# A recurrent stage with one PSUM bank for each gate and a single set of banks, rows set behind their chain's last step, and a first sample in four buffers

## The chip, the cores and the metric

The kernel runs on one core of one Trainium2 chip. The metric is the device time of one execution in microseconds (us), given as the median of several runs. Kernels are compared by the ratio of their fast runs on the same chip in the same rounds. A profile is one execution taken by the hardware profiler. Its times agree with the timed runs, but one profile differs from the next, mostly late in the program where nothing was changed: from the first difference of the adder convolution (explained below) to the end, the 14 profiles of this case take 6934 to 6973 us. So the argument uses marks inside the first 960 us, and the medians for the whole. All runs were in the fast state.

## The reference, cut to what matters

The program is four layers in a chain on an input of 16 x 32 x 128 x 128, each with a group normalisation before it and a residual after it. The change touches layer 0 and the beginning of layer 1.

```python
# layer 0: a recurrence over the 128 columns of the skewed image
xs = skewed input, moved so that one step is one column            # (128, 16, 128, 128)
def step(carry, xt):
    pc, ph = carry
    ph_shift = pad(ph, one row down)
    g = xt + einsum(W1_prev, ph_shift) + einsum(W1_cur, ph) + b1
    o, f, i, gg = sigmoid, sigmoid, sigmoid, tanh of the four quarters of g
    nc = f * pc + i * gg
    nh = o * tanh(nc)
    return (nc, nh), nh
x = x + scan(step)(_gn(x))
# layer 1: input quantised to 8 bits, then an "adder" convolution
qx = round(clip(_gn(x) / scale, -127, 127))
y  = -sum over the 3 x 3 x 32 patch of |patch - weight|
x = x + y * scale
# layers 2 and 3 (a Hartley convolution and a small U-net) are not touched
```

In step t only the first t + 1 rows have their own input; the rows below are all alike. So the kernel computes only `rows` rows, more with every eight steps.

## The kernel before

The batch of 16 samples is worked on as four groups of 128 partitions (4 samples x 32 channels). Two groups make one **chain**, so there are two independent chains, and the kernel takes a step of one, then of the other. Eight steps are a **chunk**; within a chunk the number of rows is fixed: 10 in the first chunk, 18 in the second, 128 in the last. A tile of one chain step is two groups wide, so at 98 rows the profile shows 196 columns. A **bank** is a piece of PSUM, the memory that TensorE's products go to; here each bank holds two gates of a chain.

One chain step is: TensorE makes 8 products of the input (`xn`) and 16 of the last state (8 of `h`, 8 of `e`, a copy of `h` with its two halves of partitions exchanged), all on 64 x 64 tiles of the array. (The trace has two matmul records for each of these products: 4096 of `xn` for 256 chain steps of 8.) ScalarE takes four gates. VectorE makes the cell and, after ScalarE's tanh of the cell, `h` and `e`.

```python
    T = 8
    F, I, G, O = range(4)
    BANK = ((I, F), (O, G))
    ...
        def add(ch, res, g, half):                 # residual and its statistics, once for each step
            ...
            nc.vector.tensor_add(r, r, h[:, :, 1 : n + 1])
            if n < H:
                r = res[:, g, steps, n:]
                nc.vector.tensor_add(r, r, bcast(h[:, :, n], 2, H - n))
            nc.vector.bn_stats(stat1[:, g, 2 * ch + half, :], ...)
            ...
        with tc.tile_pool(name="s0_gps", bufs=2, space=PSUM) as gps:
            for ch in range(NT):
                n = rows(ch)
                following = load(ch + 1) if ch + 1 < NT else None
                if ch:                             # rows that come in with this chunk
                    m = rows(ch - 1)
                    for c in range(2):
                        for v in (hs[c][(ch - 1) % 2][:, T - 1, :, 1:], ex[c][0][:, :, 1:], cs[c]):
                            if n > m:
                                nc.vector.tensor_copy(v[:, :, m:n], bcast(v[:, :, m - 1], 2, n - m))
                for j in range(T):
                    t = T * ch + j
                    for c in range(2):
                        ...
                        pg = gps.tile([128, 2, 2, 2, H], F32, name=f"pg{c}")   # two banks, two gates in each
                        place = {q: pg[:, i, k] for i, b in enumerate(BANK) for k, q in enumerate(b)}
                        ...                        # 8 products of xn, then 16 of h and e
                        for q in (F, I, G, O):
                            nc.scalar.activation(gt[:, q, :, :n], place[q][:, :, :n], ...)
                        nc.vector.tensor_mul(cell, cell, gt[:, F, :, :n])
                        nc.vector.tensor_mul(ig[:, :, :n], gt[:, I, :, :n], gt[:, G, :, :n])
                        nc.vector.tensor_add(cell, cell, ig[:, :, :n])
                        nc.scalar.activation(th[:, :, :n], cell, AF.Tanh)
                        nc.vector.tensor_mul(h_out[:, :, 1 : n + 1], gt[:, O, :, :n], th[:, :, :n])
                        for half in range(2):      # e: the halves of h exchanged
                            nc.vector.tensor_copy(ex[c][(t + 1) % 2][own, ...], h_out[other, ...])
                    if j >= T // 2:
                        add(ch, res, j - T // 2, 0)
                        if following:
                            normalise(ch + 1, following[0], j - T // 2)
                    elif ch:
                        add(ch - 1, previous, j, 1)
```

This is the source order. Unless it is told otherwise, the compiler chooses the order in which each engine's queue holds the instructions. The kernel has a helper, `keep_order`, which ties each instruction to the one before it on its engine. Before and after, it is not used in this stage.

The next stage quantises sample 0 in four pieces, with two buffers for the pieces and two for the quantised results, writes them to memory and reads the whole map back from there:

```python
        for i in range(4):
            t = self.unquantised(0, i)     # load a 512 KB piece
            self.scaled(0, t)              # ScalarE
            self.quantise(0, i, t)         # VectorE, then a store to memory
            weave.due(float("inf"))
        before, following = None, self.loaded(0, 0)    # the map
```

## Time and profile before

| mark of the profile before | us |
|---|---|
| median of the timed runs given with it (3 runs, 7895.84 to 7903.62) | 7900.34 |
| span of the profile | 7884.7 |
| recurrent stage: first tanh begins | 104.5 |
| first four chunks (10 to 34 rows) | 155.3 |
| chunk at 98 rows | 51.51 |
| last `h` begins | 837.15 |
| first load of sample 0 issued | 839.98 |
| map of sample 0 issued | 900.78 |
| first difference of the adder convolution begins | 934.73 |

The length of a chunk is counted from the first tanh of the cell in it to the first in the next; tiles of each chunk have their own width, so the trace tells them apart.

The page gives the busy share of each engine in 40 equal slices, in tenths. In the views PE is TensorE, PEld its weight loads, DVE VectorE, ACT ScalarE, and SPq the queue that issues transfers. A slice is 7884.7 / 40 = 197 us, so the recurrent stage and the first sample lie in the first five digits.
```profile
PE   3788366566677668886676666897667765997797
DVE  7787599989969797887877978888787877134213
```
The reader is to see that no engine of this stretch stands at 9, and that the fifth digit dips: 3 for TensorE and 5 for VectorE. That dip, at 788 to 985 us, holds the wait for the first sample.

### The profile page before, as it was taken

The numbers are of one execution on the slowest core, as the hardware profiler recorded it, in microseconds if no ns is written. First come the engines' busy times: TensorE is split into PE (matmuls) and PEld (weight loads), VectorE is DVE, ScalarE is ACT, GpSimd is POOL, SyncE is SP. The second block draws the span as 40 slices with busy tenths as digits, with TensorE's granted clock in tenths as the row PEclk, the third lists the DMA queues.
The fourth block names the chain that finished last, engine by engine and source line by source line (L and its number), as shares of the span: only waits on it lengthen the run. The fifth ranks groups of instructions, "written<-read, shape, count | busy, mean of one in ns | idle before, by whom it ended". The sixth has DMA issues, their size and how long they took to land. (4 is left out here: it accounts for less than half of the span.)

```text
span 7884.7 us, 258419 instructions
## 1 busy us (share of the span) xinstructions
PE 5635.8 (71%) x121132; PEld 3165.4 (40%) x121132; DVE 5847.9 (74%) x7177; ACT 5406.7 (69%) x3129; POOL 21.6 (0%) x15
## 2 busy tenths in 40 slices
PE   3788366566677668886676666897667765997797
PEld 3665222222253334442343343343335333555564
DVE  7787599989969797887877978888787877134213
ACT  2565488799869879887778877887887885123122
POOL 0000000000000000000000000000000000000000
PEclk9899788888878779998868788998787887897896
DMA  8653111111132431112332432120333233434314
GB/s 319 223 181 130 59 50 60 48 52 39 50 116 80 123 102 51 58 33 67 79 98 90 129 89 73 40 70 34 88 86 101 87 102 94 116 107 122 91 33 90
DMA packets 374269, 721.68 MB, mean 92 GB/s; under 512 B 50896, under 2 KB 219856, under 8 KB 362320
## 3 DMA queue, kind: packets, MB, share of 16 engines
q1 hardware_dynamic: 372768, 704.58, 29.4%
q8 instruction: 949, 15.55, 0.8%
q14 instruction: 120, 0.98, 0.0%
q10 hardware_dynamic: 432, 0.57, 0.0%
HBM read 507.21 MB, written 164.32 MB: 85 GB/s over the span
## 5 line engine op out<-in xcount | busy, mean ns | idle before, releaser
L610 ACT ACTIVATE d_act<-q,neg 128x8192 f16<-128x8192 f16 (+1 forms) x612 | 4332.5, 7137 | 930.9 <-PE acc L536 877.6
L614 DVE TENSOR_SCALAR d_dve<-q,qw 128x8192 f16<-128x8192 f16 (+1 forms) x1692 | 3906.2, 2361 | 512.0 <-PE acc L536 476.3
L536 PE MATMUL acc<-d_dve,sel 128*32 128x512 f16 x27072 | 2007.5, 432 | 861.6 <-DVE d_dve L614 838.8
L536 PEld LDWEIGHTS <-sel 128*32 128x32 f16 x36864 | 1121.1, 106 | 2800.6 <-issue 2196.8
L536 PE MATMUL acc<-d_act,sel 128*32 128x512 f16 x9792 | 784.5, 446 | 499.1 <-ACT d_act L610 494.7
L1519 PE MATMUL acc<-xp,wf 32*32 32x512 f32 x25600 | 986.0, 625 | 29.0 <-issue 16.1
L1519 PEld LDWEIGHTS acc<-xp,wf 32*32 32x32 f32 x25600 | 478.8, 105 | 378.1 <-issue 244.6
L1458 ACT ACTIVATE y<-pooled,b 32x128 f32<-32x128 f32 x512 | 204.6, 400 | 532.2 <-DVE pooled L1444 525.1
L223 PE MATMUL pg<-h,wb 64*64 64x20 f32 (+15 forms) x4096 | 401.2, 323 | 102.4 <-DVE h L255 67.0
L753 PE MATMUL acc<-y,u_conv 32*32 32x256 f32 (+1 forms) x9728 | 402.2, 511 | 79.3 <-issue 35.8
L223 PE MATMUL pg<-e,wb 64*64 64x20 f32 (+15 forms) x4096 | 353.2, 318 | 24.7 <-DVE e L258 10.0
L243 ACT ACTIVATE gt<-pg,bias 128x20 f32<-128x20 f32 (+15 forms) x1024 | 302.7, 377 | 84.2 <-PE pg L223 80.0
L1204 PE MATMUL acc<-xp 32*64 32x204 f32 (+3 forms) x8576 | 247.3, 368 | 130.0 <-ACT xp L1170 107.8
L552 PE MATMUL acc<-q,sel 32*32 32x512 f16 x4608 | 158.6, 556 | 204.9 <-DVE xr L519 115.1
L223 PEld LDWEIGHTS pg<-h,wb 64*64 64x64 f32 x4096 | 243.7, 156 | 140.5 <-DVE h L255 97.6
L223 PEld LDWEIGHTS pg<-e,wb 64*64 64x64 f32 x4096 | 250.6, 158 | 108.3 <-DVE e L258 77.9
L223 PE MATMUL pg<-xn,wb 64*64 64x8 f32 (+60 forms) x4096 | 267.9, 304 | 25.3 <-ACT gt L243 17.4
L1616 ACT ACTIVATE xr<-xr,l_ms 128x1024 f32<-128x1024 f32 x64 | 70.4, 1141 | 305.6 <-DVE xr L1611 254.3
L753 PEld LDWEIGHTS acc<-y,u_conv 32*32 32x32 f32 x9728 | 189.7, 119 | 220.0 <-issue 126.5
L1164 ACT ACTIVATE xp<-xp,fr_shift,stats 128x1280 f32<-128x1280 f32 (+1 forms) x128 | 181.7, 1431 | 136.1 <-DMA xp<-x_d 73.9
L1204 PEld LDWEIGHTS acc<-xp 32*64 32x64 f32 (+1 forms) x8576 | 199.3, 147 | 187.8 <-ACT xp L1170 118.0
L254 ACT ACTIVATE th<-c 128x20 f32<-128x20 f32 (+15 forms) x256 | 81.9, 320 | 222.2 <-DVE c L252 221.2
(203 smaller groups left out, 4247.9 us busy)
## 6 DMA issues: line engine op xcount, KB each, us to landing
xr<-x_d SPq DMA_DIRECT2D x192, 512.0 KB
xp<-x_d SPq DMA_DIRECT2D x112, 640.0 KB
q<-q_d SPq DMA_DIRECT2D x32, 2145.0 KB
x_d<-xr SPq DMA_DIRECT2D x128, 512.0 KB
x_in<-in_x_dram SPq DMA_DIRECT2D x16, 2048.0 KB
res<-in_x_dram SPq DMA_DIRECT2D x64, 512.0 KB
xn<-in_xs_dram SPq DMA_DIRECT2D x64, 512.0 KB
xn<-xn SPq DMA_DIRECT2D x128, 256.0 KB
```

The source lines that it names most:

```text
L223: nc.tensor.matmul(place[q][64 * pair : 64 * pair + 64, :, :width], wb[half, 4 * kind + KIND[q]].rearrange("p b o -> p (b o)"), v[half], s ...
L243: nc.scalar.activation(gt[:, q, :, :n], place[q][:, :, :n], AF.Tanh if q == G else AF.Sigmoid, bias=bias[:, KIND[q] : KIND[q] + 1],)
L254: nc.scalar.activation(th[:, :, :n], cell, AF.Tanh)
L536: self.nc.tensor.matmul(acc[k][32 * j : 32 * j + 32, :], self.sel16[:, i // 9, :], d[:, row : row + 4, c : c + W], start=False, stop=i == 71,)
L552: self.nc.tensor.matmul(acc[k][32 * j : 32 * j + 32, :], self.sel16[rows, 8, :], q[rows, row : row + 4, kw : kw + W], start=tap == 0, stop ...
L610: nc.scalar.activation(dst, src, AF.Relu, bias=self.neg[:, i : i + 1])
L614: nc.vector.tensor_scalar(dst, src, self.qw[:, i : i + 1], 0.0, ALU.subtract, ALU.max)
L753: nc.tensor.matmul(acc[blk][32 * j : 32 * j + 32, o : o + rows * n], t[part, 4 * par + tap, :], src[part, top : top + rows, left : left + ...
L1164: nc.scalar.activation(v, v, AF.Identity, bias=shift[0], scale=self.stats3[:, 1])
L1204: nc.tensor.matmul(gram[blk][j : j + width, at : at + n], xp[part, l, 2 + j : 2 + j + width], xp[part, rows, j : j + width + 4], start=sta ...
L1458: nc.scalar.activation(d, s, AF.Identity, bias=bj)
L1519: nc.tensor.matmul(acc[blk][32 * j : 32 * j + 32, :], tap_of("all", tap)[rows], xp[rows, 4 * j + kh : 4 * j + kh + 4, kw : kw + W], start= ...
```

## The change

It has several parts. Each gate gets a bank of its own, F and I are produced first, and so ScalarE can begin while TensorE still writes G and O. Since one set for both chains now takes eight banks, as many as two sets took before, the input products of a chain's next step are placed behind the other chain's step. The rows that come in with a chunk are set right after their own chain's last step instead of at the seam, and the next chunk is normalised two steps sooner. And the first sample's four loads go out at once into four buffers.

```diff
-    BANK = ((I, F), (O, G))
+    PAIRS = ((F, I), (G, O))
 ...
-        with tc.tile_pool(name="s0_gps", bufs=2, space=PSUM) as gps:
+        with tc.tile_pool(name="s0_gps", bufs=1, space=PSUM) as gps:
+            bank = [[gps.tile([128, 2, 256], F32, name=f"pg{c}_{q}") for q in range(4)] for c in range(2)]
+            def product(c, kind, q, copy, pair, v, width): ...      # into bank[c][q]
+            def inputs(c, t, xn): ...                               # 8 products of xn for chain c, step t
+            inputs(0, 0, xn)
             for ch in range(NT):
 ...
-                if ch:                                              # copies of rows at the seam
-                    ...
+                        for gates in PAIRS:
+                            for kind in range(2):                   # h, then e
+                                for copy, q in enumerate(gates):
+                                    for pair in range(2):
+                                        product(c, kind, q, copy, pair, v, n)
+                        if c == 0:
+                            inputs(1, t, xn)
+                        elif t + 1 < W:
+                            inputs(0, t + 1, xn if j + 1 < T else following[0])
 ...
+                        if j == T - 1 and n < H:
+                            m = rows(ch + 1)
+                            for v in (h_out[:, :, 1:], e_out[:, :, 1:], cs[c]):
+                                nc.vector.tensor_copy(v[:, :, n:m], bcast(v[:, :, n - 1], 2, m - n))
+                    if following and 2 <= j < 6:
+                        normalise(ch + 1, following[0], j - 2)
                     if j >= T // 2:
                         add(ch, res, j - T // 2, 0)
-                        if following:
-                            normalise(ch + 1, following[0], j - T // 2)
 ...
-        for i in range(4):
-            t = self.unquantised(0, i)
-            self.scaled(0, t)
-            self.quantise(0, i, t)
-            weave.due(float("inf"))
+        with tc.tile_pool(name="s1_x0", bufs=4, side="right") as pool:
+            xq = [self.unquantised(0, i, pool) for i in range(4)]
+            for i in range(4):
+                self.scaled(0, xq[i])
+                self.quantise(0, i, xq[i])
+                weave.due(float("inf"))
```

More of the change, by code (lines that the diff above doesn't have):

```diff
@@ L199, in stage0, with product, inputs @@
             normalise(0, xn, g)
-        with tc.tile_pool(name="s0_gps", bufs=2, space=PSUM) as gps:
+        with tc.tile_pool(name="s0_gps", bufs=1, space=PSUM) as gps:
+            bank = [[gps.tile([128, 2, 256], F32, name=f"pg{c}_{q}") for q in range(4)] for c in range(2)]
+            def product(c, kind, q, copy, pair, v, width):
+                half = slice(64 * (pair ^ copy), 64 * (pair ^ copy) + 64)
+                nc.tensor.matmul(
+                    bank[c][q][64 * pair : 64 * pair + 64, :, :width],
+                    wb[half, 4 * kind + KIND[q]].rearrange("p b o -> p (b o)"),
+                    v[half],
+                    start=kind == 2,
+                    stop=kind == 1,
+                    skip_group_check=True,
+                )
+            def inputs(c, t, xn):
+                for gates in PAIRS:
+                    for copy, q in enumerate(gates):
+                        for pair in range(2):
+                            v = xn[copy][:, 2 * c : 2 * c + 2, t % T, : t + 1]
+                            product(c, 2, q, copy, pair, v, t + 1)
+            inputs(0, 0, xn)
             for ch in range(NT):
@@ L203, in stage0 @@
                 following = load(ch + 1) if ch + 1 < NT else None
-                if ch:
-                    m = rows(ch - 1)
-                    for c in range(2):
-                        for v in (hs[c][(ch - 1) % 2][:, T - 1, :, 1:], ex[c][0][:, :, 1:], cs[c]):
-                            if n > m:
-                                nc.vector.tensor_copy(v[:, :, m:n], bcast(v[:, :, m - 1], 2, n - m))
                 for j in range(T):
@@ L215, in stage0 @@
                         h_out, cell = hs[c][ch % 2][:, j], cs[c][:, :, :n]
-                        pg = gps.tile([128, 2, 2, 2, H], F32, name=f"pg{c}")
-                        place = {q: pg[:, i, k] for i, b in enumerate(BANK) for k, q in enumerate(b)}
-                        def product(kind, k, i, pair, v, width):
-                            q = BANK[i][k]
-                            half = slice(64 * (pair ^ i), 64 * (pair ^ i) + 64)
-                            nc.tensor.matmul(
-                                place[q][64 * pair : 64 * pair + 64, :, :width],
-                                wb[half, 4 * kind + KIND[q]].rearrange("p b o -> p (b o)"),
-                                v[half],
-                                start=kind == 2 and k == 0,
-                                stop=kind == 1,
-                                skip_group_check=True,
-                            )
-                        for k in range(2):
-                            for i in range(2):
-                                for pair in range(2):
-                                    product(2, k, i, pair, xn[i][:, 2 * c : 2 * c + 2, j, : t + 1], t + 1)
-                        for k in range(2):
+                        for gates in PAIRS:
                             for kind in range(2):
-                                for i in range(2):
+                                for copy, q in enumerate(gates):
                                     for pair in range(2):
-                                        product(kind, k, i, pair, h_in[i][:, :, 1 - kind : n + 1 - kind], n)
+                                        v = h_in[copy][:, :, 1 - kind : n + 1 - kind]
+                                        product(c, kind, q, copy, pair, v, n)
[3 more added lines that the diff above has]
+                            inputs(0, t + 1, xn if j + 1 < T else following[0])
                         gt = gp.tile([128, 4, 2, H], F32, name=f"gt{c}")
@@ L244, in stage0 @@
                                 gt[:, q, :, :n],
-                                place[q][:, :, :n],
+                                bank[c][q][:, :, :n],
                                 AF.Tanh if q == G else AF.Sigmoid,
@@ L255, in stage0 @@
                         nc.vector.tensor_mul(h_out[:, :, 1 : n + 1], gt[:, O, :, :n], th[:, :, :n])
+                        e_out = ex[c][(t + 1) % 2]
                         for half in range(2):
                             own, other = slice(64 * half, 64 * half + 64), slice(64 - 64 * half, 128 - 64 * half)
-                            nc.vector.tensor_copy(ex[c][(t + 1) % 2][own, :, 1 : n + 1], h_out[other, :, 1 : n + 1])
+                            nc.vector.tensor_copy(e_out[own, :, 1 : n + 1], h_out[other, :, 1 : n + 1])
+                        if j == T - 1 and n < H:
[4 more added lines that the diff above has]
+                        normalise(ch + 1, following[0], j - 2)
                     if j >= T // 2:
                         add(ch, res, j - T // 2, 0)
-                        if following:
-                            normalise(ch + 1, following[0], j - T // 2)
                     elif ch:
@@ L477, in __init__, with unquantised @@
             )
-    def unquantised(self, b, i):
-        t = self.xp.tile([128, 8 * W], F32, name="xq")
+    def unquantised(self, b, i, pool=None):
+        t = (pool or self.xp).tile([128, 8 * W], F32, name="xq")
         self.nc.sync.dma_start(t, jc_rows(self.d["x1"], b, i // 2, 8 * (i % 2), 8))
```

## The prediction

> **What bounds the kernel now.** I began with the page. Its slices show three busy engines and no single bound over the whole span, so the place of the change decides. The line groups put every line of the diff except one into the first 840 us: the recurrent stage (its last h is written at 837.2 us) and, at 840 to 935 us, the loading and quantising of the first sample of the next stage. The other 6950 us run the same instructions before and after; I take them as unchanged.
>
> The second view is the timeline of VectorE in the recurrent stage, here where a step is 2 x 98 rows wide. Columns: start, duration, engine, line, operation, tiles, shape, count, and in brackets the idle time before it and what ended it.
> ```profile
> 601.83 0.53 DVE L258 COPY e<-h 64x196 f32<-64x196 f32 x2
> 602.39 0.36 DVE L250 TENSOR_TENSOR c<-c,gt 128x196 f32<-128x196 f32 x1
> 602.67 0.35 DVE L251 TENSOR_TENSOR ig<-gt 128x196 f32<-128x196 f32 x1
> 603.06 0.36 DVE L252 TENSOR_TENSOR c<-c,ig 128x196 f32<-128x196 f32 x1
> 603.92 0.36 DVE L255 TENSOR_TENSOR h<-gt,th 128x196 f32<-128x196 f32 x1 [0.49 <-ACT th L254]
> 604.38 0.53 DVE L258 COPY e<-h 64x196 f32<-64x196 f32 x2
> 604.94 0.36 DVE L250 TENSOR_TENSOR c<-c,gt 128x196 f32<-128x196 f32 x1
> ```
> From one L250 to the next is 604.94 - 602.39 = 2.55 us, one step of one of the two chains. No bracket stands before L250 or L251: VectorE does not wait for a gate here. It waits once, 0.49 us for the tanh of the cell; all else is its own six instructions, in order, the two chains taking turns. So in the wide steps **VectorE's order is the bound**, not the gates.
>
> The third view, the timeline of PE and ScalarE around it, shows what the change wants to shorten.
> ```profile
> 602.41 0.38 PE L223 MATMUL pg<-e,wb 64*64 64x196 f32 x2
> ...
> 603.62 0.33 PE L223 MATMUL pg<-e,wb 64*64 64x196 f32 x2
> ...
> 604.06 1.37 ACT L243 ACTIVATE gt<-pg,bias 128x196 f32<-128x196 f32 x4 [0.18 <-PE pg L223]
> ```
> The four gates start at 604.06, only when the last product has ended (603.62 + 0.33 = 603.95). They are done with F by 604.06 + 1.37/4 = 604.40, and VectorE takes F at 604.94: 0.5 us of slack already.
>
> The fourth view is the table of waits of VectorE from 95 to 841 us: total us, times, longest.
> ```profile
> DVE h L255 <- ACT th L254: 85.9, 196, 1.4
> DVE c L250 <- ACT gt L243: 36.3, 39, 9.3
> DVE ig L251 <- ACT gt L243: 4.7, 26, 0.3
> ```
> Waits for gates are 41.0 us in all, of which 9.3 is the one at the very start. The same table by stretches puts 19.4 + 2.9 + 5.1 + 6.6 = 34.0 us of the 36.3 before 320 us, in steps at most about 50 rows wide. That caps what faster gates can give: 41.0 - 9.3 = about **32 us**.
>
> The fifth view is the timeline after the stage: one 512 KB piece of the first sample after another.
> ```profile
> 855.30 0.56 SPq L482 DMA_DIRECT2D xq<-x_d  x1
> 867.35 1.24 ACT L486 ACTIVATE xq<-xq,shift,r 128x1024 f32<-128x1024 f32 x1 [13.95 <-DMA xq<-x_d]
> 868.62 0.69 DVE L493 TENSOR_SCALAR qt<-xq 128x1024 f16<-128x1024 f32 x1 [11.98 <-ACT xq L486]
> ...
> 870.47 0.53 SPq L482 DMA_DIRECT2D xq<-x_d  x1
> ...
> 900.78 0.53 SPq L505 DMA_DIRECT2D q<-q_d  x1
> ```
> Each load is issued only after the store of an earlier piece on the same issuing queue, and that store waits for its quantised piece. A round is 870.47 - 855.30 = 15.2 us, of which 12.05 us (855.30 to 867.35) is the load. All compute engines stand idle meanwhile; this time is on the path.
>
> **What the Trainium skill says.** (1) "PSUM — Partial Sum Buffer", section "Summary: rules for kernel authors": read PSUM during matmuls from a different bank, and guard by bank. One bank per gate allows F to be read while G is written. The trace before shows the opposite arrangement: ScalarE starts after the last product. (2) Same page, section "Engine vs sequencer instructions": the queues of ScalarE and VectorE are strict FIFO. The trace agrees: F is done at 604.40, but its multiply starts at 604.94, after the two copies ahead of it; so an earlier F does not move it. (3) "TensorEngine Tiling (Array Packing)", section "Key Properties": tiles work in parallel. The trace agrees: h and e products run in each other's time. (4) "DMA: Bandwidth & Descriptors", section "Why a DMA increments its semaphore by 16 and not by 1": a transfer runs on the largest number of engines, up to 16, that divides its slowest dimension on both sides, the lowest-numbered ones on this issuing path. These loads have a slowest dimension of 4 in memory, so 4 engines, always the same. The windows table agrees: a DMA share of 0.25 whether one or two transfers are in flight.
> ```profile
> 860.00:862.00 2.00, 0.00 (x0) 0.00 (x0) 0.00 (x0) 0.00 (x0) 0.00 (x0) 0.50 0.25 92
> 862.00:864.00 2.00, 0.00 (x0) 0.00 (x0) 0.00 (x0) 0.00 (x0) 0.00 (x0) 0.50 0.26 104
> ```
> The last two columns are DMA share and GB/s.
>
> **The change part by part.**
>
> *One bank per gate, F and I first.* The 16 recurrent products of a chain step stay 16, the 8 input products 8, the activations 4. F's and I's products end half-way: at 98 rows the products after e take 603.95 - 602.41 = 1.54 us, so F can start about 0.7 us sooner, and since F and I no longer stand in front of G, G ends near one activation (0.34 us) after its products instead of three (1.03 us). The loop of a single chain shrinks by 0.7 us or a little more. But the compiled order of VectorE is nearly the same: h follows directly on the cell's add 172 times before and 177 times after, and F's multiply directly on a copy of e 163 and 159 times. From 58 rows on PE's order is regular in both programs as well. In the wide steps the 0.7 us go into slack: **0 us**. In the narrow steps, up to about 50 rows, some of the 32 us of gate waits go. There the compiled order is rougher than before: runs of four h products on the same two tiles, then four e products (50 runs of four at 10 rows, 8 at 50, none from 58), where the kernel before always alternates in twos. That loses tile parallelism. I choose a bit under half: **14 us** of 32.
>
> *Inputs behind the other chain's step, a single set of banks.* They now wait for that gate's activation of the same chain's last step. In the wide steps PE has about 0.4 us idle per 2.55 us, and the activations end well before the next h of that chain. **0 us**, with risk in the narrow steps (counted in the choice above).
>
> *Rows set behind their chain's last step.* 90 copies before (30 for each of c, h and e, 165 to 178 ns each), 15 seams x 2 chains x 3 = 90 after: nothing is saved, they move. PE's weight loads waited 39.1 us for such copies, but these waits lie at the seams of chunks beside VectorE's adds. **0 to 3 us**; I count 0.
>
> *Normalising two steps earlier.* Moves 64 activations of 0.84 us median on ScalarE, which has room. **0 us**.
>
> *First sample in four buffers.* Removes three waits for a free buffer and queue place. It does not remove bytes: four loads of 524 KB and four stores of 266 KB on the same four engines. In the compiled order loads 2 to 4 stand behind the issue of the weights' load (846.9 us) and the zero rows, so they can be issued from about 847 to 850. Until the quantised map can be loaded, loads 2, 3, 4 and stores 1, 2, 3 must pass: 3 x 0.524 + 3 x 0.266 = 2.37 MB. Rate: between 856 and 866 the kernel before moved one load and one store, 0.79 MB, in 9.7 us = 81 GB/s; peaks are 104. So 23 to 29 us, plus 2 us that I allow for the last store to land: the map's load goes out at about 847 + 26 + 2 = 875 instead of 900.78. **26 us**.
>
> Sum: 14 + 26 = 40 us, 7900.34 - 40 = 7860.
>
> **The rivals.** (a) *The stage is latency-bound throughout, and each step gains 0.7 us per chain loop*: 128 steps x 0.7 = 90 us, with the first sample 7785. For it: ScalarE waits 221.2 us for the cell. Against it: no gate wait of VectorE beyond 320 us worth more than 1 us, and the unchanged order. (b) *The single set of banks becomes a new wait*: PE, in order, stands before an input product for an activation while the other chain's products queue behind. If 0.3 us were lost in each of some 80 narrow chain steps, 24 us go and the stage loses 10: 7884. For it: the compiled order puts such inputs between the h and e products in narrow steps. Against it: VectorE's own copies of e (0.36 us) hide most of it. (c) *The loads just queue on their four engines and the gain vanishes*: at 81 GB/s or less with the map's first load pushed behind piece 4, gain about 15: 7871. (d) *Loads spread well, and ScalarE and VectorE alone bound the pieces* (1.24 + 1.13 us each): the map goes out near 860, gain 40: 7846.
>
> **Range and chances.** Low: gates 25 and first sample 40 plus a few us from the seams, 7832. High: gates 0, first sample 15, 7886. Runs before differ by 8 us. A gain over 2% would need 158 us, more than VectorE's 126.9 us of waits listed above and the first sample's part together can plausibly give; a loss over 2% has no part to come from. Faster 0.02, same 0.97, slower 0.01.
>
> **What would show it.** After: steps at 98 rows still 2.5 to 2.6 us from F's multiply to the next, with ScalarE's F and I now starting while PE still writes G and O; h still waiting about 0.5 us for the tanh, about 80 to 90 us in all; waits of F's multiply for gates down from 36 to some 22 us; the stage ending near 823 instead of 837 us; the map's load issued 35 to 45 us after the first piece's load instead of 61, DMA share 0.25 throughout. I am wrong if the wide step gets shorter than 2.4 us (VectorE's order was not the bound), if VectorE's gate waits grow (rival b), or if the map goes out less than 15 us sooner relative to the first load.

## The result

The changed kernel took **7879.22 us** in the median (7872.24 to 7884.26, 4 runs) against 7898.16 us for the kernel before (7895.84 to 7903.62, 4 runs). The ratio is 0.9974, with a 95% interval of 0.9957 to 0.9992. Here and below a ratio is the mean time of one kernel's fast runs over that of the other's of the same rounds, so it is not quite the ratio of the medians. The outcome is inside the range of the prediction, but the gain is 19 us where 40 had been predicted.

The views that the prediction used, now of the changed kernel. First VectorE's timeline at 98 rows (start, duration, engine, line, operation, tiles, shape, count, idle time before it and what ended it):
```profile
600.97 0.36 DVE L251 TENSOR_TENSOR c<-c,gt 128x196 f32<-128x196 f32 x1
...
602.50 0.36 DVE L256 TENSOR_TENSOR h<-gt,th 128x196 f32<-128x196 f32 x1 [0.49 <-ACT th L255]
...
603.53 0.36 DVE L251 TENSOR_TENSOR c<-c,gt 128x196 f32<-128x196 f32 x1
```
A step is 603.53 - 600.97 = 2.56 us against 2.55, and the only wait in it is still 0.49 us for the tanh. Then TensorE and ScalarE in the same step:
```profile
602.10 0.37 ACT L255 ACTIVATE th<-c 128x196 f32<-128x196 f32 x1 [0.92 <-DVE c L253]
602.21 0.33 PE L207 MATMUL pg<-e,wb 64*64 64x196 f32 x2
...
602.37 1.35 ACT L244 ACTIVATE gt<-pg,bias 128x196 f32<-128x196 f32 x4
```
The gates begin at 602.37, before the last product of `e` ends (602.21 + 0.33 = 602.54). So the new layout does what it is meant to do, but by only 0.17 us: ahead of the gates stands the other chain's tanh, for which ScalarE waits 0.92 us. VectorE takes F at 603.53, 1.16 us after the gates have begun.

VectorE's waits from 95 to 841 us (total us, times, longest):
```profile
DVE h L256 <- ACT th L255: 83.1, 188, 0.8
DVE c L251 <- ACT gt L244: 23.9, 40, 2.9
DVE ig L252 <- ACT gt L244: 22.0, 46, 3.3
```
The waits of F's multiply fell from 36.3 to 23.9 us, but those of the multiply of I and G rose from 4.7 to 22.0, so the waits for gates went from 41.0 to 45.9 us in all. The wait at the very start has to be taken out of these sums before they are compared. Before, it is one wait of F, 9.3 us; after, it stands in three pieces, at 96.95 and 100.04 us for F (2.43 and 2.91 us) and at 103.56 us for I and G (3.33 us). Without it F's waits fell from 27.0 to 18.6 us, those of I and G rose from 4.7 to 18.7, and the sum from 31.7 to 37.2 us.

The first sample, from the timeline:
```profile
842.11 0.59 SPq L489 DMA_DIRECT2D xq<-x_d  x1
...
861.42 15.84 SPq L505 DMA_DIRECT2D q_d<-qt  x4
...
869.91 1.24 ACT L493 ACTIVATE xq<-xq,shift,r 128x1024 f32<-128x1024 f32 x1 [3.78 <-DMA xq<-x_d]
...
880.12 0.54 SPq L512 DMA_DIRECT2D q<-q_d  x1
...
917.61 9.21 DVE L622 TENSOR_SCALAR d_dve<-q,qw 128x8192 f16<-128x8192 f16 x4 [39.86 <-DMA q<-q_d]
```
The last piece is scaled at 869.91, and the map goes out at 880.12, which is 38.0 us after the first load instead of 60.8. From its issue to its use the map then takes 917.61 - 880.12 = 37.5 us, where it had taken 934.73 - 900.78 = 33.9. DMA share and GB/s stand last in the table of windows:
```profile
862.00:864.00 2.00, 0.00 (x0) 0.00 (x0) 0.96 (x6) 0.00 (x0) 0.00 (x0) 0.50 0.26 106
```
The share is 0.26 although two loads and one or two stores are in flight: still four of the sixteen engines.

| mark, us | before | after | difference |
|---|---|---|---|
| first four chunks (10 to 34 rows) | 155.3 | 162.6 | +7.3 |
| from there to the last `h` | 577.3 | 572.6 | -4.7 |
| chunk at 98 rows | 51.51 | 51.34 | -0.2 |
| last `h` begins | 837.15 | 839.24 | +2.1 |
| from the last `h` to the first difference | 97.6 | 78.4 | -19.2 |
| from there to the end | 6950 | 6953 | +3 |

So the whole gain lies behind the last `h`. The recurrent stage did not get shorter.

### The profile page after: what moved, and what is told of

Read it like the earlier page. It is cut to its first block, busy times and chain, and to the rows that moved or that the text cites. A ratio compares the mean times of both kernels' runs of the same rounds, so it can differ in the third digit from the quotient of the medians.

```text
span 7870.4 us, 258146 instructions
## 1 busy us (share of the span) xinstructions
PE 5674.4 (72%) x121132; PEld 3192.7 (41%) x121132; DVE 5847.9 (74%) x7177; ACT 5407.7 (69%) x3129; POOL 21.9 (0%) x15
## 5 line engine op out<-in xcount | busy, mean ns | idle before, releaser
L207 PE MATMUL pg<-xn,wb 64*64 64x28 f32 (+61 forms) x4096 | 285.0, 302 | 9.8 <-ACT gt L244 3.3
```

Source lines behind the costliest of these rows:

```text
L207: nc.tensor.matmul(bank[c][q][64 * pair : 64 * pair + 64, :, :width], wb[half, 4 * kind + KIND[q]].rearrange("p b o -> p (b o)"), v[half], ...
```

## The experiments

Two theories stood at the beginning. **Theory**: the 14 us that had been expected in the narrow steps are really there, and the compiled order of TensorE's products eats them; the wide steps are bound by VectorE's order. **Rival**: the single set of banks is a wait of its own (rival b of the prediction), or the two chains are bound by their own latency, so that nothing on VectorE helps.

All kernels below gave correct results. Each was timed in rounds with the kernel before, whose medians were 7896.1 us in the first two jobs, 7871.0 in the job of the ninth and tenth and 7877.7 in that of the last two. The columns to the right come from one profile each.

| kernel | median us (runs) | ratio to before, 95% interval | first four chunks | chunk at 98 rows | last `h` begins | last `h` to first difference |
|---|---|---|---|---|---|---|
| before | | 1 | 155.3 | 51.51 | 837.15 | 97.6 |
| after | 7879.22 (4) | 0.9974, 0.9957 to 0.9992 | 162.6 | 51.34 | 839.24 | 78.4 |
| e1_first4 | 7874.24 (9) | 0.9973, 0.9963 to 0.9983 | 155.6 | 52.63 | 844.01 | 77.4 |
| e2_recurrent | 7899.78 (13) | 1.0000, 0.9991 to 1.0009 | 162.0 | 51.36 | 840.21 | 96.9 |
| e3_pe_order | 7854.80 (5) | 0.9947, 0.9935 to 0.9960 | 141.2 | 51.34 | 816.46 | 78.5 |
| e4_spread16 | 7853.14 (5) | 0.9939, 0.9926 to 0.9951 | 162.0 | 51.36 | 840.23 | 43.6 |
| e5_all_order | 7895.96 (13) | 0.9998, 0.9990 to 1.0007 | 151.8 | 52.46 | 859.71 | 77.7 |
| e6_fill | 7783.37 (4) | 0.9856, 0.9841 to 0.9871 | 131.1 | 44.66 | 740.91 | 78.7 |
| e7_fill_spread | 7741.59 (4) | 0.9804, 0.9788 to 0.9820 | 129.2 | 44.66 | 739.52 | 43.4 |
| e8_step_order | 7875.83 (7) | 0.9975, 0.9964 to 0.9985 | 153.5 | 51.33 | 833.89 | 76.0 |
| e9_before_fill | 7887.66 (15) | 1.0019, 1.0011 to 1.0026 | 150.4 | 54.49 | 857.18 | 96.7 |
| e10_act_free | 7724.62 (4) | 0.9823, 0.9803 to 0.9843 | 133.4 | 44.63 | 751.00 | 43.1 |
| e11_early_norm | 7814.27 (5) | 0.9920, 0.9908 to 0.9933 | 135.8 | 47.27 | 777.84 | 96.5 |
| e12_old_banks | 7783.38 (4) | 0.9875, 0.9860 to 0.9890 | 135.3 | 44.68 | 748.89 | 96.2 |

### Each half alone: e1_first4 and e2_recurrent

The first is the kernel before with only the first sample in four buffers; the second is the changed kernel with the first sample as before.

```diff
 # e1: the kernel before plus
+        with tc.tile_pool(name="s1_x0", bufs=4, side="right") as pool:
+            xq = [self.unquantised(0, i, pool) for i in range(4)]
 # e2: the changed kernel minus the same lines
```

> The kernel before with only the first sample in four buffers. My theory: the whole gain of the change is here. In the changed kernel the time from the last h of the recurrent stage to the first difference fell from 934.7 - 837.2 = 97.5 us to 917.6 - 839.2 = 78.4 us, so this run should be 17 to 21 us faster than before (ratio 0.9973 to 0.9979). Rival (the gain is shared by both parts and a clock difference hides the rest): 8 to 12 us faster.

> The changed kernel with the first sample loaded as before, so the recurrent part alone. My theory: between 0 and 5 us slower than before (the last h of the stage came at 839.2 us instead of 837.2), with the first four chunks of eight steps near 162 us instead of 155 and the later ones shorter or equal. Rival: 8 to 12 us faster.

The first sample alone gives 0.9973, the same as the whole change; the recurrent part alone gives 1.0000. The two profiles agree: 77.4 and 96.9 us behind the last `h`. The narrow loss repeats too: 155.6 us where the recurrent code is the old one, 162.0 where it is the new one. A warning lies in the last `h` of e1: the same recurrent code as before ended it at 844.0 instead of 837.2, with longer chunks from 164 columns on (52.63 against 51.51 us at 98 rows). The instructions of VectorE and ScalarE stand in the same order in both profiles. So a few us in the wide chunks of one profile mean nothing.

### The order of TensorE: e3_pe_order and e8_step_order

In e3 the source order is kept on TensorE throughout the recurrent stage. In e8 it is kept only among the 16 products of one chain step; the compiler may still mix chains and input products.

```diff
-def keep_order(nc, tc, start):
+def keep_order(nc, tc, start, engines=None):
 ...
+        if engines and i.engine not in engines:
+            continue
 ...
+            start = len(nc.cur_bb.bb.instructions)     # e8: before each chain step's products
             inputs(0, 0, xn)
             for ch in range(NT):
 ...
+            keep_order(nc, tc, start, (mybir.EngineType.PE,))   # e8: after each chain step's products
```

> The changed kernel with TensorE alone held to the order of the source in the recurrent stage (h and e products alternating in twos, the chains in turn); VectorE and ScalarE still ordered by the compiler. If the compiled order of TensorE (h runs before e runs) makes the loss in the narrow steps, the first four chunks fall from 162.6 us to 156 or less and the whole is 6 us or more faster than the changed kernel, 24 us or more faster than before. If the single set of banks makes it, they stay at 160 us or more.

> The changed kernel with only the 16 recurrent products of each chain step held to the order of the source (h and e in twos); which chain comes when, and the input products, stay with the compiler. If the runs of h products before e products make the loss in the narrow steps, the first four chunks fall from 162.6 us to 145 or less, near the 141.2 of the run with TensorE's whole order held, and the whole is 15 us or more faster than the changed kernel. If it was the mixing of the chains and inputs, they stay above 150.

With the order kept, the first four chunks take 141.2 us: 21.4 less than in the changed kernel and **14.1 less than before**. The table of windows shows where they come from. Columns: window, us, busy us of TensorE (count), of its weight loads, of VectorE, ScalarE and GpSimd, the granted clock, DMA share, GB/s. The kernel before, the changed one and e3, from the first tanh to the fifth chunk:
```profile
104.00:260.00 156.00, 114.81 (x3084) 101.77 (x3084) 111.13 (x502) 75.77 (x340) 0.00 (x0) 0.94 0.69 230
```
```profile
104.00:267.00 163.00, 141.31 (x3076) 127.44 (x3076) 113.41 (x505) 87.06 (x337) 0.00 (x0) 0.92 0.68 217
```
```profile
104.00:245.00 141.00, 102.36 (x3104) 91.41 (x3108) 108.20 (x498) 73.53 (x336) 0.00 (x0) 0.92 0.72 241
```
For the same number of products TensorE is busy 141 us in the changed kernel and 102 us in e3. The products are the same, and one record takes 283 and 281 ns in the mean; what differs is how many of them run beside one another. Most of it lies in the input products. The same view for them alone, of the changed kernel and of e3 (columns: window, us, TensorE, weight loads, ScalarE, clock, DMA share, GB/s):
```profile
104.00:267.00 163.00, 76.57 (x1028) 61.03 (x1028) 9.02 (x16) 0.92 0.68 217
```
```profile
104.00:245.00 141.00, 48.55 (x1036) 44.43 (x1036) 9.26 (x16) 0.92 0.72 241
```
They keep TensorE busy 76.6 us against 48.6 in e3 and 57.8 in the kernel before, while the `h` products take 75.7, 76.5 and 78.2 us and the `e` products 68.8, 66.6 and 68.5 (each kind by itself; kinds overlap). At 18 rows, 12 records of one shape (64x22) follow one another in 0.84 us in the changed kernel and in 0.59 us in e3. The timeline at 18 rows shows what this does to the gates. In the kernel before, F's multiply and that of I and G in one step:
```profile
148.96 0.20 DVE L250 TENSOR_TENSOR c<-c,gt 128x36 f32<-128x36 f32 x1 [0.53 <-ACT gt L243]
149.32 0.20 DVE L251 TENSOR_TENSOR ig<-gt 128x36 f32<-128x36 f32 x1 [0.17 <-ACT gt L243]
```
In the changed kernel:
```profile
149.09 0.75 PE L207 MATMUL pg<-h,wb 64*64 64x36 f32 x10 [0.36 <-DVE h L256]
...
150.16 0.20 DVE L251 TENSOR_TENSOR c<-c,gt 128x36 f32<-128x36 f32 x1 [0.66 <-ACT gt L244]
150.82 0.20 DVE L252 TENSOR_TENSOR ig<-gt 128x36 f32<-128x36 f32 x1 [0.46 <-ACT gt L244]
```
The records of `h` products come in a run of ten, and those of `e` behind it partly in runs of four, where the kernel before mostly alternates the two by twos. The four activations of the step are stretched to 1.13 us by waits for products (0.83 us in the step shown of before), and the multiply of I and G, which stands behind the third of them, waits 0.46 us. In e3 VectorE's waits for gates fall to 23.8 us, of which the multiply of I and G has 2.1 and that of F 21.7, 8.8 of it at the start.

e8 missed its number: 153.5 us instead of 145 or less. It recovers 9.1 of the 21.4 us. The rest, 12.3 us, needs the order between the chains and the input products too, since that is all in which the edits of e8 and e3 differ. By e8's own expectation ("above 150") the mixing of chains and input products is thus the larger part, which fits the 28 us of busy time above.

That e3 is 14.1 us shorter than the kernel **before** does not show what the new banks are worth. The kernel before with TensorE's order held and nothing else was not run, and its own compiled order keeps TensorE busy 114.8 us, also more than e3's 102.4. The only pair with the old and the new arrangement in which every order is held alike is e12 and e6, below: there the first four chunks take 135.3 and 131.1 us, a difference of 4.2.

The single set of banks, rival (b), is in e3 as well, and the loss is gone there. The page of the changed kernel already speaks against it. Groups of input products, with busy us, mean ns, idle us before them and what ended most of it, before and after:
```profile
L223 PE MATMUL pg<-xn,wb 64*64 64x8 f32 (+60 forms) x4096 | 267.9, 304 | 25.3 <-ACT gt L243 17.4
```
```profile
L207 PE MATMUL pg<-xn,wb 64*64 64x28 f32 (+61 forms) x4096 | 285.0, 302 | 9.8 <-ACT gt L244 3.3
```
The waits of input products for a gate to have been read fell from 17.4 to 3.3 us and those of all weight loads for a gate from 21.0 to 9.8 (in e3 they are 0.7 and 0.9), although there is only one set of banks.

### More DMA engines for the first sample: e4_spread16

Each transfer of the first sample (four loads, four stores, the map) is split into four of 32 partitions, whose slowest dimension is 32 instead of 4.

```diff
+    def by_block(self, out, src):
+        for a in range(4):
+            p = slice(32 * a, 32 * a + 32)
+            ...                       # src or out without its outermost dimension, at block a
+            self.nc.sync.dma_start(out[p], src_a)
 ...
-        self.nc.sync.dma_start(t, v)
+        self.by_block(t, v)           # likewise the stores and the first map
```

> The changed kernel with each transfer of the first sample (four loads, four stores, the load of the map) issued as four transfers of 32 partitions, so that each may run on all DMA engines instead of four. If the four engines bound this stretch (about 40 us to the map's issue and 37 us for the map), the first difference starts at 870 to 885 us instead of 917.6 and the whole is 30 to 45 us faster than the changed kernel, 50 to 65 us faster than before. If the chain of load, scale, quantise and store bounds it, under 10 us faster than the changed kernel. DMA share should rise from 0.25 to 0.6 or more in bursts.

The first difference begins at 883.84 us instead of 917.61, as expected, and the median falls from 7879 us (or 7874 in e1, of the same job) to 7853. That is 26 us below the changed kernel and 43 below the kernel before, short of the 30 to 45 and 50 to 65 expected. A window of the profile of e4:
```profile
858.00:862.00 4.00, 0.28 (x8) 0.20 (x8) 1.60 (x6) 2.48 (x2) 0.00 (x0) 0.50 1.07 247
```
The DMA share is 1.07 (0.26 in the changed kernel; the view can exceed 1) at 247 GB/s, and the map, issued at 870.57, takes 883.84 - 870.57 = 13.3 us instead of 37.5. So after the change the four DMA engines are the bound of the first sample; the four buffers had only removed the waiting between their transfers.

### What bounds the wide steps: e5_all_order, e6_fill, e7_fill_spread

In e5 TensorE, ScalarE and VectorE all keep the source order. In e6, on top of that, the residual's adds are cut in two parts and put right behind the tanh's issue: the two adds in the wait of chain 0, the statistics in that of chain 1. e7 is e6 with the transfers of e4.

```diff
+            keep_order(nc, tc, start, (PE, Activation, DVE))          # e5
 ...
                         nc.scalar.activation(th[:, :, :n], cell, AF.Tanh)
+                        if j >= T // 2:                               # e6: part 0 adds, part 1 bn_stats
+                            add(ch, res, j - T // 2, 0, c)
+                        elif ch:
+                            add(ch - 1, previous, j, 1, c)
                         nc.vector.tensor_mul(h_out[:, :, 1 : n + 1], gt[:, O, :, :n], th[:, :, :n])
 ...
-                    if j >= T // 2:
-                        add(ch, res, j - T // 2, 0)
-                    elif ch:
-                        add(ch - 1, previous, j, 1)
```

> The changed kernel with TensorE, ScalarE and VectorE all held to the order of the source in the recurrent stage, the adds of a finished half chunk after each step of both chains. It is the control for the next run. VectorE's wide step stays 2.5 to 2.6 us at 98 rows, plus 1.3 us of adds per step of both chains, so the stage ends within 8 us of the run with only TensorE's order held (816 us): 35 to 50 us faster than before. If strict turns hurt the narrow steps, the stage ends later than 825 us.

> The same order, but the adds of a finished half chunk cut in two and put where VectorE waits for the tanh of the cell (85 us of such waits in the stage). If VectorE's order is the bound (my theory), the waits for the tanh almost go and the stage ends 60 to 85 us sooner than in the control; the chunk at 98 rows takes 43 to 46 us instead of 51. If the chains' latency is the bound (rival: each chain needs its own 5 us from h to h), h comes later, the time comes back as waits for gates, and the gain is under 20 us.

> The filled waits together with the first sample's transfers spread over all DMA engines. The two lie one after the other in time, so their gains add: 25 to 30 us faster than the filled run alone, 115 to 155 us faster than before.

e5 was a miss: I had expected it to be faster, and its last `h` came 20 us later than in the changed kernel. VectorE waited for the tanh in each of the 256 chain steps:
```profile
DVE h L257 <- ACT th L256: 114.6, 256, 0.8
```
In the compiled order of the changed kernel 188 are left. In the other 68 something else stands right before `h`: in 34 of them an add or a statistic of the residual, in the others an instruction of the chains' steps. Held to source order, the adds stood behind the steps, and every wait was paid. e6, planned together with e5, puts the adds into the waits on purpose.

e6's VectorE at 98 rows, from its timeline:
```profile
511.20 0.36 DVE L255 TENSOR_TENSOR c<-c,gt 128x196 f32<-128x196 f32 x1
...
512.15 0.69 DVE L192 BATCH_NORM_STATS2 stat<-res 128x6 f32<-128x512 f32 x1
512.75 0.34 DVE L264 TENSOR_TENSOR h<-gt,th 128x196 f32<-128x196 f32 x1
...
513.75 0.36 DVE L255 TENSOR_TENSOR c<-c,gt 128x196 f32<-128x196 f32 x1
```
The step is still 513.75 - 511.20 = 2.55 us, as long as in the kernel before, but the statistics are in it, in the place where `h` had waited; no bracket is left. The other chain's step, with the two adds in it, takes 2.64 us. The chunk falls from 52.46 to 44.66 us and the last `h` comes at 740.91 instead of 859.71 us, 119 us sooner than in e5 and 98 sooner than in the changed kernel. The expectation had been 60 to 85 us against e5, from the 85 us of such waits in the compiled order; e5 had lost 114.6. VectorE's waits for the tanh are down from 114.6 us to
```profile
DVE h L264 <- ACT th L259: 2.9, 9, 0.3
```
while those for gates are 24.9 us for F (8.8 at the start) and 13.6 for I and G.
Had the chains' own latency been the bound, moving work into the wait would have moved little: that rival had expected under 20 us and fell. VectorE's in-order queue is the bound of the wide steps. e7 adds the two findings: 7741.59 us, with 0.9804 the lowest ratio of the study. It is 36.7 us sooner than e6 at the first difference and 41.8 in the medians, more than the 25 to 30 expected.

### Are the banks worth anything once VectorE doesn't stall? e9 to e12

e9 is the kernel **before**, with its banks and its first sample, held to source order and filled as e6. e11 is e9 with the next chunk normalised two steps sooner, e12 is e11 with the rows set behind their chain's last step: both as the change has them. e10 is e7 with ScalarE's order left to the compiler.

```diff
 # e11 = e9 and
-                    if following and j >= T // 2:
-                        normalise(ch + 1, following[0], j - T // 2)
+                    if following and 2 <= j < 6:
+                        normalise(ch + 1, following[0], j - 2)
 # e12 = e11 and
-                if ch:
-                    ...                     # copies of rows at the seam
+                        if j == T - 1 and n < H:
+                            ...             # the same copies behind the chain's own last step
 # e10 = e7 and
-            keep_order(nc, tc, start, (PE, Activation, DVE))
+            keep_order(nc, tc, start, (PE, DVE))
```

> The kernel before with its own banks and its own first sample, but with the same two edits as the filled kernel: TensorE, ScalarE and VectorE held to source order in the recurrent stage, and the adds of the residual put into the two waits for the tanh. It asks whether one bank for each gate is worth anything once VectorE no longer stalls. Theory (VectorE's own work bounds the wide steps, the gates have slack in either layout): the last h at 745 to 765 us (filled kernel with the new banks 740.9), the chunk at 98 rows within 0.7 us of 44.66, only the narrow steps longer; median 7790 to 7830 (the first sample is the slow one, about 19 us). Rival (with the tanh wait gone, the gates come up as the next limit and the layout is worth its 0.7 us in each of 128 steps): the last h at 800 to 835 us, waits for gates over 80 us in all, median above 7850.

> The filled kernel with the split transfers, but only TensorE and VectorE held to source order; ScalarE is left to the compiler's order. Theory (ScalarE is not the bound and its order matters little as long as the tanh is not behind a normalisation): the last h within 6 us of 739.5, median 7735 to 7750. Rival (the normalisations, 0.84 us each, now fall in front of a tanh or a gate): the last h 10 us or more later, and waits of h for the tanh of over 10 us.

> The filled kernel with the old banks missed: its last h came at 856.7 us. Its trace shows two stalls of VectorE at every seam of two chunks, at 196 rows 3.2 and 6.3 us: TensorE, held to source order, waits for the copied rows of chain 0, which stand behind chain 1's last step, and then for the transfer that mirrors the last normalised quarter, which is issued about 9 us before it lands. This kernel is that one with the normalising moved two steps earlier, as the change has it. Theory (that transfer is the larger stall): the gap of about 6 us at each seam goes, the chunk at 98 rows falls from 54.49 to 47.5 to 49 us, the last h comes at 765 to 795 us. Rival (the bank layout is what costs): the last h stays above 830 us.

> The same with the rows also set behind their chain's last step, as the change has it. What then differs from the filled kernel is the layout of the banks, the order of the gates' products, the place of the input products and the first sample. Theory (seams alone; the bank layout is worth nothing in wide steps): the chunk at 98 rows within 0.7 us of 44.66, the last h at 740 to 755 us, median about 19 us above the filled kernel's gain, a ratio of 0.987 to 0.990. Rival (one bank for each gate is worth 0.3 us or more in each step once VectorE does not stall): chunk at 98 rows above 47 us, last h above 765 us.

e9 missed by 90 us, and by its numbers the rival had more than won: the last `h` at 857.18 (the rival had said 800 to 835), VectorE's waits of F's multiply 134.6 us. Yet the waits were only 59, far fewer than the 256 chain steps. Its timeline at the seam to the chunk of 98 rows:
```profile
574.33 0.59 PE L227 MATMUL pg<-h,wb 64*64 64x196 f32 x2 [3.75 <-DVE h L214]
...
577.85 0.36 DVE L254 TENSOR_TENSOR c<-c,gt 128x196 f32<-128x196 f32 x1 [3.19 <-ACT gt L247]
```
```profile
582.56 0.66 PEld L227 LDWEIGHTS pg<-xn,wb 64*64 64x64 f32 x10 [5.33 <-DMA xn<-xn]
```
```profile
587.16 0.36 DVE L254 TENSOR_TENSOR c<-c,gt 128x196 f32<-128x196 f32 x1 [6.34 <-ACT gt L247]
```
TensorE first stands 3.75 us for the copied rows (line 214), which in source order come behind the other chain's last step. Then it waits 5.33 us for the transfer that exchanges the halves of the last normalised group. VectorE loses 3.19 + 6.34 = 9.5 us at this seam; the chunk is 54.49 - 44.66 = 9.8 us longer than e6's. So the step is not longer, the seam is.

e11 and e12 show it. Normalising sooner alone takes the last `h` from 857.18 to 777.84 (79 us), the rows behind their chain's step another 29, to 748.89. And with the old banks, two gates in each, the chunk at 98 rows is 44.68 us against 44.66 with one bank for each gate. The layout is worth **nothing in the wide steps, even when VectorE does not stall**. What is left to the whole new arrangement of banks, products and inputs is 748.89 - 740.91 = 8.0 us, over half of it (135.3 - 131.1 = 4.2) in the first four chunks and 1.4 before the first tanh. This comes from one profile of each, on different chips, and the timed runs do not show it: the ratios 0.9875 and 0.9856 lie some 15 us apart, and the first sample alone makes up 96.2 - 78.7 = 17.5.

The prediction had counted 0 for the rows and 0 for the normalising. In the compiled order nothing speaks against that: the chunk at 98 rows, its seam included, is 51.51 us before and 51.34 after. Where the source order is held, the two are worth 108 us together, and the timed ratios agree (1.0019 and 0.9875, some 113 us).

e10 settles nothing. Its profile fits its rival (last `h` at 751.0, 17.9 us of waits for the tanh), but its timed runs do not show the 11 us: the intervals of its ratio (0.9803 to 0.9843) and of e7's (0.9788 to 0.9820) overlap. The profiled execution was also the slowest of its four, 7761.44 us, where the others took 7720.76 to 7727.58.

## Why the prediction was right or wrong

**Right: the wide steps gain nothing, because VectorE's order is the bound.** The step at 98 rows stayed (2.55 and 2.56 us), and e6 shows the cause: filling the tanh's wait shortens the stage by 119 us against e5, whereas earlier gates shorten the wide chunks not at all (e12 against e6). The size of the earlier start was off: the prediction had F start 0.7 us sooner, but the gates moved only from 0.11 us behind the last product's end to 0.17 us ahead of it, since the other chain's tanh stands in front of them in ScalarE's own queue. That cost nothing, since those 0.7 us were booked as slack. The Trainium skill's page "PSUM — Partial Sum Buffer", section "Engine vs sequencer instructions", names the strict FIFO of both queues; the trace agrees for ScalarE: it stood idle for 0.92 us until the tanh's cell was ready, and the gates behind it then began without a wait, where before they had waited 0.18 us for a product. One reading was loose: TensorE's "about 0.4 us idle per 2.55 us" is a mean over 570 to 620 us, seams included (41.78 of 50 us busy); within the step it is busy 2.47 of 2.55 us. Rivals (a) and (d) fell: the step did not shrink below 2.4 us, and the map went out at 880 and not near 860.

**Wrong: 14 us in the narrow steps.** The failed step is "I choose a bit under half: 14 us of 32". The first four chunks became 7.3 us longer, and the stage ended at 839 us where 823 had been forecast. The prediction had seen one cause, the runs of four `h` products, and had judged it smaller than the gain. Keeping the order within each step (e8) gives back only 9.1 of the 21.4 us by which the compiled order is behind the source order (e3). The other 12.3 go with the order between chains and input products, and the input products were booked at "0 us", with a risk counted into the 14. What the gain without this loss would be is not shown: that e3 is 14.1 us below before is no proof of the predicted 14, since e3 also holds an order which the kernel before does not have; with all orders held alike the new arrangement is worth 4.2 us in these chunks (e6 against e12). The prediction also watched F alone. F's waits came to 23.9 us, where it had said some 22, but part of that fall is the start wait in pieces: without it F gained 8.4 us and the multiply of I and G lost 14.0.

**Rival (b) had the sign, not the reason.** The waits for gates grew, which the prediction had named as the mark of (b). But the single set of banks is not the cause: it stays in e3, where the loss is gone, and the input products' waits for gates fell from 17.4 to 3.3 us.

**Right in its mechanism, too large: 26 us from the first sample.** The map was to go out at about 35 us after the first load and did so at 38.0, which is 22.8 us sooner than before. Some 3.5 us were then given back, because the map took 37.5 us instead of 33.9. This repeats in every profile with four buffers and unsplit transfers (35.2 to 37.7 us, against 33.6 to 34.0 with two). Why it takes longer was not tested. During the map the four engines are equally busy in both profiles (share 0.25), but they move 72 GB/s after and 81 before. That it still shares them with the last stores does not explain it: before, the map is issued 0.7 us after the last store; after, 3.4 us after it, once a store has landed. The cause stays open. The term measures 19.2 us in the profiles of before and after, 20.2 in e1, and a ratio of 0.9973 in e1's timed runs.

**Right: the four engines stay the bound**, as rival (c) also held. The share stayed at 0.26, and e4 shows what spreading the transfers over more engines was worth: 34 us at the first difference. (c)'s size did not come true: it had the first sample gain about 15 us.

The sum in its place: instead of 14 + 26 = 40 us, the profiles show -2 + 19 = 17, beside 19 in the medians. So the whole gain is the first sample's, and the 14 us were not there.

## What to carry to other kernels

Before making an operand come sooner, look at what stands ahead of its reader in the reader's own queue: a step that is bound by an in-order engine was shortened here by filling that engine's waits with work it had to do anyway, and not by operands that came sooner and then stood in line. A change of layout also changes the order which the compiler chooses, so compare the compiled orders, and try the source order on one engine at a time: the same products took 141 or 102 us of TensorE. For a transfer on the path, look at the DMA share before adding buffers: where it stood at 4 of 16 engines here, the shape of the transfer was the limit (the map took 37.5 us, and 13.3 when split).

## What the Trainium skill lacked or had wrong

- "TensorEngine Tiling (Array Packing)", section "Key Properties", says that tiles execute in parallel. The runs agree, but the page does not say that the order of the instructions decides how far they do, and I found no page that measures it: about 3,100 matmul records on 64 x 64 tiles kept TensorE busy 141.3 us in one order and 102.4 us in another.
- "PSUM — Partial Sum Buffer", section "Summary: rules for kernel authors", advises to read from a different bank than the one being written, or at least a different quadrant. The page means it as a guard against collisions and gives no measure of what it is worth in time. Here one bank for each gate was worth nothing at 98 rows (44.66 us, against 44.68 with two gates in each) and, with all that goes with it, 8.0 us of the whole stage in one pair of profiles.
- "DMA: Bandwidth & Descriptors", section "Why a DMA increments its semaphore by 16 and not by 1", gives the rule of how many engines a transfer uses, and which ones, and the runs agree: share 0.26 at 106 GB/s for a slowest dimension of 4, with several transfers in flight, and 1.07 at 247 GB/s for 32. What it lacks is the size of the effect: here splitting nine transfers was worth 34 us at the first difference.
- I found no page on putting independent work into an in-order engine's waits. It was the largest effect of the study: 119 us of the stage against the same order unfilled (e5), and 98 us against the changed kernel.
